# Strassen sums of a small weight written column block by column block, and a new order of work in the last block of queries

## The chip, the cores and the metric

The kernel runs on one core of a Trainium2 chip. The metric is the device time of one execution in microseconds (us); lower is better. All arithmetic is float32.

## The reference, cut to what matters

The layer is a gated cross-attention followed by an RMS norm. `x` is 8 x 1024 x 1024, the context 8 x 64 x 512, `W_mem` 1024 x 512, `W_gate` 1024 x 2048.

```python
memory_proj = einsum('bme,de->bmd', memory, W_mem)
scores = einsum('bnd,bmd->bnm', hidden_states, memory_proj) / sqrt(D)
attn = softmax(scores)
memory_context = einsum('bnm,bmd->bnd', attn, memory_proj)
gate = sigmoid(einsum('bnf,df->bnd', concat([hidden_states, memory_context]), W_gate) + b_gate)
fused = hidden_states + gate * memory_context
return fused * rsqrt(mean(fused ** 2) + 1e-6) * norm_w
```

The two large products are `memory_proj` (the setup) and the half of the gate that multiplies `hidden_states` (the main loop). The other half of the gate is folded into the setup: `memory_proj` is multiplied by the second half of `W_gate` once.

## The kernel before, in words

**Setup (about the first 82 us).** `W_mem` arrives transposed in the tile `wm`, four row blocks of 128 (the contraction) by 1024 output features. The feature of chunk j, position m is column `8*m + j`, so that the columns of one chunk lie 8 elements (32 bytes) apart. `transpose_mem(g)` transposes the context on TensorE into `memT`, VectorE and ScalarE copying half of the results each (L199). The product is one level of Strassen in the Winograd form, seven products of `pm_product`, each of 8 matmuls (the trace has two records for each): `split` gives the four blocks w11, w12 (row blocks 0-1 and 2-3, chunks 0-3) and w21, w22 (chunks 4-7). VectorE forms the left sums `ps1` = w21+w22, `ps2` = ps1-w11, `ps3` = w11-w21, `ps4` = w12-ps2 with the helper `tt` (L95); in the trace ps1 to ps3 are `pm_s`, ps4 and the right sums `pt1`, `pt2` are `pm_it`, and the results of the products (`pm`) are added into `mpT` and `pm_t`. The products run in the order 1 (w11), 2 (w12), 5 (ps1), 6 (ps2), 7 (ps3), 3 (ps4), 4 (w22). The weights of a matmul are

```python
mm(o, l[:, k, :, j], r[:, k, :], j % 2 == 0 and k == 0, k == 1)
```

with `l` laid out as `[P, 2, P, KH]` (k, m, j): for a sum the 128 columns of a weight load lie 4 elements (16 bytes) apart, for a block read straight from `wm` 8 elements (32 bytes). Then follow seven `mg_product`s (`pg` in the trace) of `memory_proj` with the second half of `W_gate`. Meanwhile SyncE's queue stores `mpT` (`mpd`), loads the first block of `x` (`load_xq`, tile `xq`, which takes over the memory of `wm`), and VectorE transposes it into the tiles `a` (L333).

**Main loop (16 blocks of 512 rows, "quads" q).** Each quad is seven outer Strassen products in `ORDER` 1, 6, 7, 5, 4, 2, 3, each of seven inner products in "slots" named A, B, C, D, A again, E, F (tiles kA to kF). A quad has 49 slots. `at(slot, fn)` hangs a piece of other work on a slot: it is emitted just before that slot's matmuls. So the order of instructions on each engine is fixed by hand, and each engine works through its own list in that order. Within an outer product ScalarE copies kA to `u` (L783) and VectorE adds kB, kC, kD to it (`u<-u,kB` and so on); the second A product writes kA again and so waits for that copy. The last four outer products (5, 4, 2, 3) also form the attention context `pc` (rows d = odd and c = even tiles of 128 rows) and finish the gate: `sigmoid` on ScalarE, then `gated` on VectorE (multiply by `pc`).

**The last quad** finishes differently. `last_gated` multiplies by `pc`, adds `x` (tile `xl`), and has ScalarE square and sum half a row block (`junk`, L701); `last_root` adds the two half sums on VectorE and takes the root on ScalarE (`halves`, L707); `last_norm` takes the reciprocal, scales (L717) and stores. `sqrt_table()` loads the root's function table ahead of its last use.

**In the first quad** VectorE also forms the sums of the weight blocks of outer products 2 and 3 (`inner_sum`, `it<-w`, four 128x512 operations for each), at slots 3 to 6 and 10 to 13. The softmax of the quad's scores lies at slots 10 (`softmax_a`) and 13 (`softmax_b`), and TensorE transposes its result (`pa`, L427) at slot 18.

Of the kernel before, what the change touches and what calls it, by code (L numbers as in the profile page):

```python
# [8 lines left out]
F32 = mybir.dt.float32  # L9
AF = mybir.ActivationFunctionType  # L10
ALU = mybir.AluOpType
# [4 lines left out]
P = 128  # L16
# [4 lines left out]
def tile_gated_cross_attention_rmsnorm(  # L21
# [42 lines left out]
    nc = tc.nc  # L64
    B, N, D = x.shape
# [5 lines left out]
    KD = D // P  # L71
    KE = E // P
    H = 512
    C = 256
# [4 lines left out]
    const = ctx.enter_context(tc.tile_pool(name="const", bufs=1))  # L79
# [4 lines left out]
    small = ctx.enter_context(tc.tile_pool(name="small", bufs=1))  # L84
# [4 lines left out]
    pin = tc.keep_in_program_order  # L89

    def mm(o, lhsT, rhs, start, stop):
        pin(nc.tensor.matmul(o, lhsT, rhs, start=start, stop=stop, skip_group_check=True))  # L92

    def tt(eng, o, a, b, op):
        pin(eng.tensor_tensor(o, a, b, op))  # L95

    def load(o, i):
        pin(nc.sync.dma_start(o, i))

    def t4k(pool, shape, tag, name):  # L100
        return pool.tile(shape, F32, tag=tag, name=name)
# [33 lines left out]
    for k in range(KD):  # L135
        t = t4k(*((gpool, [P, D], "gate") if k < 7 else (apool, [P, D], "s4")), f"w2_{k}")
# [42 lines left out]
    eps_sb = const.tile([P, 1], F32, name="eps_sb")  # L179
# [7 lines left out]
    def transpose_mem(g):  # L187

        cols = slice(g * (BM // 2), (g + 1) * (BM // 2))
        for k in range(KE):  # L190
            for r in range(2):
                n = 2 * g + r
                pin(
                    nc.tensor.transpose(
                        pt[k][:, n * P : (n + 1) * P], memq[g][:, r, k * P : (k + 1) * P], ident
                    )
                )
            o = memT[k // 2][:, k % 2, cols]
            pin((nc.scalar.copy if k % 2 else nc.vector.tensor_copy)(o, pt[k][:, cols]))  # L199
# [1 line left out]
    pt = [bank(4, [P, BM], "pt0")]  # L201
    pt += [ps_ctx.tile([P, BM], F32, tag="ctx", name=f"pt{k}") for k in (1, 2)]
    pt += [ps.tile([P, BM], F32, tag="sc", name="pt3")]
    transpose_mem(0)


    def outer_sum(o, a, b, k=slice(0, 4)):
# [13 lines left out]
    KH = KD // 2  # L221
# [6 lines left out]
    def setup_bank(name):  # L228
        nonlocal setup_next
        tag = setup_banks[setup_next % 8]  # L230
        setup_next += 1
        return (ps_ctx if tag == "ctx" else ps).tile([P, H], F32, tag=tag, name=name)

    def split(t, r):

        return t.rearrange("p k (m j) -> p k m j", j=KD)[:, :, :, KH * r : KH * (r + 1)]

    def pm_left(pool, tag, name):
        return t4k(pool, [P, 2, P, KH], tag, name)

    def pm_product(n, l, r, k_first=False):

        pgs = [setup_bank(f"pm{n}_{i}") for i in range(2)]
        order = [(j, k) for j in range(KH) for k in range(2)]
        if k_first:
            order.sort(key=lambda jk: jk[1])
        for j, k in order:
            o = pgs[j // 2][:, (j % 2) * HM : (j % 2 + 1) * HM]
            mm(o, l[:, k, :, j], r[:, k, :], j % 2 == 0 and k == 0, k == 1)
        return pgs  # L250

    def pm_sum(o, a, pgs):
        for i in range(2):
            js = slice(2 * i, 2 * i + 2)
            pg = pgs[i].rearrange("p (j n) -> p j n", n=HM)
            tt(nc.vector, o[:, js], a[:, js], pg, ALU.add)

    w11, w12 = (split(wm[:, 2 * k : 2 * k + 2, :], 0) for k in range(2))
    w21, w22 = (split(wm[:, 2 * k : 2 * k + 2, :], 1) for k in range(2))
    e11, e12 = (memT[0][:, :, c * HM : (c + 1) * HM] for c in range(2))  # L260
    e21, e22 = (memT[1][:, :, c * HM : (c + 1) * HM] for c in range(2))
    pu = const.tile([P, KH, H], F32, tag="t5", name="pm_t5")[:, :, :HM]
    ps4 = const.tile([P, 3, 2, C], F32, tag="it5", name="pm_it5")[:, :2]
    ps4 = ps4.rearrange("p a k c -> p (a k c)").rearrange("p (k m j) -> p k m j", k=2, j=KH)
    ps1 = pm_left(apool, "s1", "pm_s1")
    ps2 = pm_left(apool, "s2", "pm_s2")
    ps3 = pm_left(small, "mg", "pm_s3")
    in_it7 = const.tile([P, 3, 2, C], F32, tag="it7", name="pm_it7")
    pt1, pt2 = in_it7[:, 0], in_it7[:, 1]

    p1 = pm_product(1, w11, e11, True)
    tt(nc.vector, ps1, w21, w22, ALU.add)
    transpose_mem(1)
    for i in range(2):
        pin(
            nc.scalar.copy(
                pu[:, 2 * i : 2 * i + 2], p1[i].rearrange("p (j n) -> p j n", n=HM)
            )
        )
    pgs = pm_product(2, w12, e21)  # L280
    tt(nc.vector, pt1, e12, e11, ALU.subtract)
    tt(nc.vector, ps2, ps1, w11, ALU.subtract)
# [30 lines left out]

    pgs = pm_product(3, ps4, e22)
    pm_sum(m21, m21, pgs)
    p4 = pm_product(4, w22, e21)


    A, S, L2, O = {}, {}, {}, {}
# [1 line left out]
    def where(q, t=0):  # L321
        return q // QPB, (q % QPB) * QT + t * P
# [254 lines left out]
    def at(slot, fn, *args):  # L577
        due.setdefault(slot, []).append(lambda: fn(*args))

    def mid(key, fn, *args):  # L580
        beside.setdefault(key, []).append(lambda: fn(*args))
# [40 lines left out]
    for o in (2, 3):  # L622
        w1_place(o)
    for i, (o, n) in enumerate((o, n) for o in (2, 3) for n in range(4)):
        at((3, 4, 5, 6, 10, 11, 12, 13)[i], inner_sum, nc.vector, o, n)
    slot = 0

    def step():
# [4 lines left out]
    def gated(q, t, h, pc):  # L633
        g = O[q, t][:, h * H : (h + 1) * H]
        tt(nc.vector, g, g, pc, ALU.mult)

    def sigmoid(q, t, h):
        g = O[q, t][:, h * H : (h + 1) * H]
        pin(nc.scalar.activation(g, g, AF.Sigmoid))  # L639
# [42 lines left out]
    xl, halves = {}, {}  # L682
# [8 lines left out]
    def last_gated(t, h, pc):  # L691
        q = NQ - 1
        gated(q, t, h, pc)
        cols = slice(h * H, (h + 1) * H)
        g = O[q, t][:, cols]
        tt(nc.vector, g, g, xl[t][:, cols], ALU.add)
        if t not in halves:
            halves[t] = t4k(small, [P, 3], f"halves{t}", f"halves{t}")
        junk = t4k(small, [P, H], "junk", f"junk_{t}_{h}")
        pin(  # L700
            nc.scalar.activation(junk, g, AF.Square, accum_out=halves[t][:, h : h + 1])  # L701
        )

    def last_root(t):
        ss = halves[t]
        tt(nc.vector, ss[:, 2:3], ss[:, 0:1], ss[:, 1:2], ALU.add)
        pin(nc.scalar.activation(ss[:, 2:3], ss[:, 2:3], AF.Sqrt, bias=eps_sb, scale=1.0 / D))  # L707

    def last_norm(t, h):
        b, n0 = where(NQ - 1, t)  # L710
        rstd = halves[t][:, 2:3]
        if h == 0:
            pin(nc.vector.reciprocal(rstd, rstd))
        cols = slice(h * H, (h + 1) * H)
        g = O[NQ - 1, t][:, cols]
        pin(
            nc.vector.scalar_tensor_tensor(g, g, rstd, nw_sb[:, cols], ALU.mult, ALU.mult)  # L717
        )
        load(out[b, n0 : n0 + P, cols], g)

    def sqrt_table():

        t = t4k(small, [P, 1], "warm", "warm")
        pin(nc.scalar.activation(t, eps_sb, AF.Sqrt))

    def outer_product(q, o, ext):
# [54 lines left out]
        p1, u2, u3, u4 = (ut[:, i, :] for i in range(4))  # L781
# [12 lines left out]
        pcs = []  # L794
        if ext:
            row, h, g = ext
# [28 lines left out]
        if ext:  # L825
            sigmoid(q, 2 * row + 1, h)
            last = q + 1 == NQ
            if last:
                at(slot + 1, last_gated, 2 * row + 1, h, pcs[1])
            else:  # L830
                at(slot + 1, gated, q, 2 * row + 1, h, pcs[1])
        product("F", 1, s4, R22, not ext)
        fin(1, "F", u4)
        if ext:
            sigmoid(q, 2 * row, h)
            if last:
                at(slot + 2, last_gated, 2 * row, h, pcs[0])
            else:
                at(slot + 2, gated, q, 2 * row, h, pcs[0])
        if o in (4, 3) and q + 1 == NQ:  # L840
            c, d = 2 * ext[0], 2 * ext[0] + 1
            if o == 3:
                sqrt_table()
            first = (4, 5) if o == 4 else (3, 3)
            at(slot + first[0], last_root, d)
            at(slot + first[1], last_root, c)
            for i, t in enumerate((d, c)):
                for h_ in range(2):
                    at(slot + first[1] + 1 + 2 * i + h_, last_norm, t, h_)
        elif o in (4, 3):  # L850

            row = ext[0]
            c, d = 2 * row, 2 * row + 1
            for t in (d, c):
                at(slot + 5, residual, q, t)
            if row == 0:
                when = (17, 18, 23, 29, None, None)
            else:
                when = (17, 18, 23, 25, 26, 28)
            at(slot + when[0], square, q, c)  # L860
            at(slot + when[1], square, q, d)
            for w_, (t, h_) in zip(when[2:], ((c, 0), (c, 1), (d, 0), (d, 1))):
                if w_ is None:
                    mid((q + 1, 4), norm, q, t, h_)
                else:
                    at(slot + w_, norm, q, t, h_)
# [7 lines left out]
    while due:  # L874
        slot = min(due)
# [27 lines left out]
```

## Time and profile before

| | |
|---|---|
| median of 3 runs | 979.76 us (979.5 to 979.79) |
| the profiled execution's own time | 979.91 us |
| its span in the profile | 978.1 us |
| granted TensorE clock, mean | 0.997 |
| busy share: TensorE matmul, weight load, VectorE, ScalarE, GpSimd | 99%, 79%, 85%, 33%, 77% |
| setup, to the first kA | 82.7 us |
| a quad of the main loop (weight loads of psT, 88.9 to 918.2 us, over 15 quads) | 55.3 us |

The profile shows one execution. Its span runs from the first to the last recorded instruction; 1.8 us of the execution's own time lie around it. Rows of a timeline give start, duration, engine, line, operation, output<-inputs, shape and count, with the idle time before and what ended it in brackets. PE is TensorE's matmuls, PEld its weight loads, DVE VectorE, ACT ScalarE, POOL GpSimd, SP the queue of SyncE.

### The profile page before, as it was taken

To read this page: it belongs to the slowest core of one execution; us is meant where nothing else is said; L and a number is where in the kernel's file an instruction comes from. 1 tells how busy PE (TensorE), PEld (TensorE's weight loads), DVE (VectorE), ACT (ScalarE), POOL (GpSimd) and SP (SyncE) were. 2 spreads that over 40 slices of the span, in tenths; PEclk is the share of its full clock that TensorE was granted. 3 is DMA by queue.
4 is the path that set the end of the run, shared out by engine and by line. 5 is a ranking of instruction groups with operands and counts; after the bars stand their busy time and mean duration, and the time that the engine had idled before them with its cause. 6 is when DMAs were issued, how large, how long until landed. Compare 5 with 4: busy or idle time off the path is not lost.

```text
span 978.1 us, 14392 instructions
## 1 busy us (share of the span) xinstructions
PE 964.3 (99%) x4986; PEld 776.3 (79%) x4986; DVE 827.0 (85%) x1487; ACT 323.0 (33%) x596; POOL 754.6 (77%) x895
## 2 busy tenths in 40 slices
PE   9999999999999999999999999999999999999995
PEld 8646888888888888888888888888888888888873
DVE  5988788979797988979797988979797988979787
ACT  1000234151423334151423334151423334151434
POOL 4986878878787878878787878878787878878772
PEclk9999999999999999999999999999999999999998
DMA  9856173482818373482819373482818373482612
GB/s 371 267 147 157 27 130 98 114 177 72 176 65 174 117 130 98 112 179 73 176 65 175 113 131 99 112 180 71 177 66 172 116 133 98 111 181 68 169 65 86
DMA packets 71255, 128.32 MB, mean 131 GB/s; under 512 B 12432, under 2 KB 49296, under 8 KB 70928
## 3 DMA queue, kind: packets, MB, share of 16 engines
q1 hardware_dynamic: 61760, 93.34, 35.1%
q0 software_dynamic: 9280, 33.56, 18.6%
q8 instruction: 39, 0.64, 0.3%
q10 hardware_dynamic: 144, 0.52, 0.2%
q14 instruction: 32, 0.26, 0.1%
HBM read 87.56 MB, written 39.85 MB: 130 GB/s over the span
## 4 chain that ended last, share of the span: by engine, by line
PE 95%; DVE 3%; DMA 1%; issue 0%; ACT 0%; POOL 0%; DVEq 0%; ACTq 0%
PE kA L92 19%; PE pc L92 12%; PE kE L92 11%; PE kF L92 10%; PE kD L92 10%; PE kC L92 10%; PE kB L92 10%; PE psT L92 6%; PE pg L92 5%; PE pm L92 3%; DVE gate L95 1%; DMA memq<-in_mem 1%; DVE gate L717 0%; PE pa L427 0%; PE sc L401 0%
## 5 line engine op out<-in xcount | busy, mean ns | idle before, releaser
L95 POOL TENSOR_TENSOR gate<-gate,u 128x256 f32<-128x256 f32 x336 | 270.3, 834 | 116.0 <-DVE u L95 110.4
L639 ACT ACTIVATE gate<-gate 128x512 f32<-128x512 f32 x128 | 79.0, 629 | 400.7 <-DVE gate L95 400.6
L95 POOL TENSOR_TENSOR l<-a 128x256 f32<-128x256 f32 x128 | 128.6, 1004 | 56.3 <-DVE a L95 55.5
L333 DVE STREAM_TRANSPOSE a<-xq 128x512 f32<-128x512 f32 x128 | 138.0, 1100 | 3.2 <-DMA mgd<-mpq 3.2
L92 PE MATMUL pc<-mg,attnT 64*128 64x256 f32 x512 | 127.4, 389 | 0.0
L668 DVE SCALAR_TENSOR_TENSOR gate<-gate,ss,nw_sb 128x512 f32<-128x512 f32 x120 | 126.2, 1061 | 1.1
L92 PE MATMUL kD<-it,l 128*128 128x256 f32 x448 | 115.0, 379 | 0.0
L92 PE MATMUL kB<-it,l 128*128 128x256 f32 x448 | 115.0, 379 | 0.0
L92 PEld LDWEIGHTS pc<-mg,attnT 64*128 64x128 f32 x512 | 90.6, 186 | 29.7 <-issue 21.2
L92 PE MATMUL kA<-w,a 128*128 128x256 f32 x384 | 98.7, 379 | 0.4 <-ACT u L783 0.4
L92 PEld LDWEIGHTS kD<-it,l 128*128 128x128 f32 x448 | 85.1, 190 | 11.6
L92 PEld LDWEIGHTS kB<-it,l 128*128 128x128 f32 x448 | 85.1, 190 | 11.6
L95 DVE TENSOR_TENSOR gate<-gate,pc 128x512 f32<-128x512 f32 x128 | 87.2, 681 | 5.8 <-ACT gate L639 5.8
L95 POOL TENSOR_TENSOR l<-s 128x256 f32<-128x256 f32 x96 | 75.6, 787 | 10.1 <-PE kF L92 10.0
L92 PEld LDWEIGHTS kA<-w,a 128*128 128x128 f32 x384 | 71.6, 190 | 10.2 <-ACT u L783 0.8
L783 ACT COPY u<-kA 128x256 f32<-128x256 f32 x112 | 40.5, 362 | 102.4 <-PE kA L92 100.4
L95 DVE TENSOR_TENSOR u<-u,kB 128x256 f32<-128x256 f32 x112 | 45.6, 407 | 28.2 <-PE kB L92 24.7
L92 PE MATMUL kE<-it,a 128*128 128x256 f32 x256 | 69.0, 392 | 0.0
L92 PE MATMUL kA<-t,s 128*128 128x256 f32 x256 | 67.4, 386 | 0.0
L92 PE MATMUL kF<-w,l 128*128 128x256 f32 x256 | 65.7, 379 | 0.0
L92 PE MATMUL kC<-w,l 128*128 128x256 f32 x256 | 65.7, 379 | 0.0
L653 ACT ACTIVATE junk<-gate 128x1024 f32<-128x1024 f32 x60 | 63.5, 1059 | 1.4 <-DMA gate<-in_x 0.5
(138 smaller groups left out, 2034.2 us busy)
## 6 DMA issues: line engine op xcount, KB each, us to landing
xq<-in_x SPq DMA_DIRECT2D x64, 512.0 KB, 9.7
gate<-in_x POOLq DMA_DIRECT2D x60, 512.0 KB, 8.2
out<-gate SPq DMA_DIRECT2D x60, 512.0 KB, 2.6
w<-in_w_gate_t SPq DMA_DIRECT2D x8, 512.0 KB, 11.0
w<-in_w_gate_t SPq DMA_DIRECT2D x2, 2048.0 KB, 17.0
mg<-mgd SPq DMA_DIRECT2D x16, 256.0 KB, 3.8
mpd<-mpT SPq DMA_DIRECT2D x4, 512.0 KB, 6.5
mgd<-mpq SPq DMA_DIRECT2D x16, 128.0 KB, 4.4
```

Source lines behind the costliest of these rows:

```text
L92: pin(nc.tensor.matmul(o, lhsT, rhs, start=start, stop=stop, skip_group_check=True))
L95: pin(eng.tensor_tensor(o, a, b, op))
L333: nc.vector.transpose(A[key][:, :, r * P : (r + 1) * P], chunks(xq[q][:, 4 * t : 4 * t + 4, :], KD)[:, half * KH : (half + 1) * KH],)
L639: pin(nc.scalar.activation(g, g, AF.Sigmoid))
L653: nc.scalar.activation(junk, O[q, t], AF.Square, accum_out=ss[:, t % 2 : t % 2 + 1])
L668: nc.vector.scalar_tensor_tensor(g[:, cols], g[:, cols], rstd[:, t % 2 : t % 2 + 1], nw_sb[:, cols], ALU.mult, ALU.mult,)
L783: pin(nc.scalar.copy(p1, kb["A"]))
```

## The change

Three things are changed.

1. **Layout of W_mem's blocks.** `split` returns the blocks as (k, j, m), and the tiles of the sums are laid out so. VectorE now reads the blocks of `wm` with a step of 32 bytes and writes the sums so that the 128 columns of one chunk are adjacent. ScalarE copies two blocks into the same layout: the first row block of w11 (`pw11`, a 128x512 copy ahead of `transpose_mem(0)`), and w22 (`pw22`, two such copies behind the copies of product 1). Product 1's second row block and product 2 still read `wm`.
2. **First quad.** The four weight sums of outer product 3 move from slots 10-13 to slots 22-25.
3. **Last quad.** `last_gated` is hung one slot later. The square of the first half of a row is followed on ScalarE by an Identity with scale 1/D and bias eps into the third column of `halves`; `last_root` is then a single root on ScalarE, with that column as its bias, and its VectorE addition is gone. Roots and norms of both row pairs get other slots.

```diff
     def split(t, r):
-        return t.rearrange("p k (m j) -> p k m j", j=KD)[:, :, :, KH * r : KH * (r + 1)]
+        return t.rearrange("p k (m j) -> p k j m", j=KD)[:, :, KH * r : KH * (r + 1), :]
     def pm_left(pool, tag, name):
-        return t4k(pool, [P, 2, P, KH], tag, name)
+        return t4k(pool, [P, 2, KH, P], tag, name)
...
-            mm(o, l[:, k, :, j], r[:, k, :], j % 2 == 0 and k == 0, k == 1)
+            mm(o, l[k][:, j, :], r[:, k, :], j % 2 == 0 and k == 0, k == 1)
...
-    transpose_mem(0)
...
-    p1 = pm_product(1, w11, e11, True)
+    in_it1 = const.tile([P, 3, 2, C], F32, tag="it1", name="pm_it1")
...
+    pin(nc.scalar.copy(pw11, w11[:, 0]))
+    transpose_mem(0)
+    p1 = pm_product(1, (pw11, w11[:, 1]), e11, True)
...
+    for k in range(2):
+        pin(nc.scalar.copy(pw22[:, k], w22[:, k]))
     pgs = pm_product(2, w12, e21)
...
-    p4 = pm_product(4, w22, e21)
+    p4 = pm_product(4, pw22, e21)
...
-        at((3, 4, 5, 6, 10, 11, 12, 13)[i], inner_sum, nc.vector, o, n)
+        at((3, 4, 5, 6, 22, 23, 24, 25)[i], inner_sum, nc.vector, o, n)
...
     def last_gated(t, h, pc):
...
+        pin(nc.scalar.activation(junk, g, AF.Square, accum_out=ss[:, h : h + 1]))
+        if h == first:
+            pin(nc.scalar.activation(ss[:, 2:3], ss[:, h : h + 1],
+                                     AF.Identity, bias=eps_sb, scale=1.0 / D))
     def last_root(t):
-        tt(nc.vector, ss[:, 2:3], ss[:, 0:1], ss[:, 1:2], ALU.add)
-        pin(nc.scalar.activation(ss[:, 2:3], ss[:, 2:3], AF.Sqrt, bias=eps_sb, scale=1.0 / D))
+        pin(nc.scalar.activation(ss[:, 2:3], ss[:, h : h + 1],
+                                 AF.Sqrt, bias=ss[:, 2:3], scale=1.0 / D))
...
-                at(slot + 1, last_gated, 2 * row + 1, h, pcs[1])
+                at(slot + 2, last_gated, 2 * row + 1, h, pcs[1])
...
-                at(slot + 2, last_gated, 2 * row, h, pcs[0])
+                at(slot + 3, last_gated, 2 * row, h, pcs[0])
...
-            first = (4, 5) if o == 4 else (3, 3)
-            at(slot + first[0], last_root, d)
-            at(slot + first[1], last_root, c)
-            for i, t in enumerate((d, c)):
-                for h_ in range(2):
-                    at(slot + first[1] + 1 + 2 * i + h_, last_norm, t, h_)
+            when = (4, 5, 7, 9, 11, 12) if o == 4 else (2, 4, 5, 6, 7, 8)
+            at(slot + when[0], last_root, d)
+            at(slot + when[1], last_root, c)
+            for w_, (t, h_) in zip(when[2:], ((d, 0), (d, 1), (c, 0), (c, 1))):
+                at(slot + w_, last_norm, t, h_)
```

More of the change, by code (lines that the diff above doesn't have):

```diff
@@ L234, in split @@
     def split(t, r):
-        return t.rearrange("p k (m j) -> p k m j", j=KD)[:, :, :, KH * r : KH * (r + 1)]
+        return t.rearrange("p k (m j) -> p k j m", j=KD)[:, :, KH * r : KH * (r + 1), :]
     def pm_left(pool, tag, name):
-        return t4k(pool, [P, 2, P, KH], tag, name)
+        return t4k(pool, [P, 2, KH, P], tag, name)
     def pm_product(n, l, r, k_first=False):
         pgs = [setup_bank(f"pm{n}_{i}") for i in range(2)]
+        if not isinstance(l, tuple):
+            l = l[:, 0], l[:, 1]
         order = [(j, k) for j in range(KH) for k in range(2)]
@@ L263, in tile_gated_cross_attention_rmsnorm @@
     ps4 = const.tile([P, 3, 2, C], F32, tag="it5", name="pm_it5")[:, :2]
-    ps4 = ps4.rearrange("p a k c -> p (a k c)").rearrange("p (k m j) -> p k m j", k=2, j=KH)
+    ps4 = ps4.rearrange("p a k c -> p (a k c)").rearrange("p (k j m) -> p k j m", k=2, j=KH)
     ps1 = pm_left(apool, "s1", "pm_s1")
@@ L269, in tile_gated_cross_attention_rmsnorm @@
     pt1, pt2 = in_it7[:, 0], in_it7[:, 1]
-    p1 = pm_product(1, w11, e11, True)
+    in_it1 = const.tile([P, 3, 2, C], F32, tag="it1", name="pm_it1")
+    pw22 = in_it1[:, :2].rearrange("p a k c -> p (a k c)").rearrange(
+        "p (k j m) -> p k j m", k=2, j=KH
+    )
+    pw11 = in_it1[:, 2].rearrange("p k c -> p (k c)").rearrange("p (j m) -> p j m", j=KH)
+    pin(nc.scalar.copy(pw11, w11[:, 0]))
+    transpose_mem(0)
+    p1 = pm_product(1, (pw11, w11[:, 1]), e11, True)
     tt(nc.vector, ps1, w21, w22, ALU.add)
@@ L697, in last_gated, with last_root @@
         if t not in halves:
-            halves[t] = t4k(small, [P, 3], f"halves{t}", f"halves{t}")
+            halves[t] = t4k(small, [P, 3], f"halves{t}", f"halves{t}"), h
+        ss, first = halves[t]
         junk = t4k(small, [P, H], "junk", f"junk_{t}_{h}")
-        pin(
-            nc.scalar.activation(junk, g, AF.Square, accum_out=halves[t][:, h : h + 1])
-        )
-    def last_root(t):
-        ss = halves[t]
-        tt(nc.vector, ss[:, 2:3], ss[:, 0:1], ss[:, 1:2], ALU.add)
-        pin(nc.scalar.activation(ss[:, 2:3], ss[:, 2:3], AF.Sqrt, bias=eps_sb, scale=1.0 / D))
+        pin(nc.scalar.activation(junk, g, AF.Square, accum_out=ss[:, h : h + 1]))
+        if h == first:
+            pin(
+                nc.scalar.activation(
+                    ss[:, 2:3], ss[:, h : h + 1], AF.Identity, bias=eps_sb, scale=1.0 / D
+                )
+            )
+    def last_root(t):
+        ss, first = halves[t]
+        h = 1 - first
+        pin(
+            nc.scalar.activation(
+                ss[:, 2:3], ss[:, h : h + 1], AF.Sqrt, bias=ss[:, 2:3], scale=1.0 / D
+            )
+        )
     def last_norm(t, h):
         b, n0 = where(NQ - 1, t)
-        rstd = halves[t][:, 2:3]
+        rstd = halves[t][0][:, 2:3]
         if h == 0:
```

## The prediction

> **What bounds the kernel now.** I read first the page's chain, then TensorE's weight loads through the setup, then VectorE beside them, and last the two ends.
>
> ```profile
> PE 95%; DVE 3%; DMA 1%; issue 0%; ACT 0%; POOL 0%; DVEq 0%; ACTq 0%
> ```
>
> TensorE is 95% of the chain. Time is gained only where TensorE runs slower than its pace, where it waits, or after its last matmul at about 967.5 us. The weight loads in order of time show the first:
>
> ```profile
> 11.80 3.91 PEld L92 LDWEIGHTS pm<-memT,wm 128*128 128x128 f32 x16
> 15.62 7.57 PEld L92 LDWEIGHTS pm<-pm_it,pm_s 128*128 128x128 f32 x32
> 23.09 3.85 PEld L92 LDWEIGHTS pm<-memT,pm_s 128*128 128x128 f32 x16
> 26.85 3.83 PEld L92 LDWEIGHTS pm<-memT,pm_it 128*128 128x128 f32 x16
> 30.59 3.93 PEld L92 LDWEIGHTS pm<-memT,wm 128*128 128x128 f32 x16
> 34.42 0.42 PEld L92 LDWEIGHTS pg<-w,mpT 128*128 128x128 f32 x2
> ...
> 84.23 0.84 PEld L92 LDWEIGHTS kC<-w,l 128*128 128x128 f32 x4
> 85.09 0.84 PEld L92 LDWEIGHTS kD<-it,l 128*128 128x128 f32 x4
> ```
>
> No idle time stands between these rows, so the distance of starts is the pace. Products 5, 6, 7, 3 take 30.59 - 15.62 = 14.97 us for 64 records, 0.234 each; product 4 takes 3.83 for 16, 0.239. The kC row, of the same shape, takes 0.86 for 4, 0.2155. The step between weight columns is the difference I see. VectorE in the setup:
>
> ```profile
> 11.29 1.22 DVE L95 TENSOR_TENSOR pm_s<-wm 128x1024 f32<-128x1024 f32 x1 [3.88 <-DMA wm<-in_w_mem_t]
> ...
> 21.66 0.69 DVE L95 TENSOR_TENSOR pm_t<-pm_t,pm 128x512 f32<-128x512 f32 x1 [0.34 <-PE pm L92]
> 23.52 0.69 DVE L95 TENSOR_TENSOR pm_t<-pm_t,pm 128x512 f32<-128x512 f32 x1 [1.18 <-PE pm L92]
> ...
> 27.28 0.69 DVE L95 TENSOR_TENSOR mpT<-mpT,pm 128x512 f32<-128x512 f32 x1 [1.19 <-PE pm L92]
> ...
> 54.09 4.10 DVE L333 STREAM_TRANSPOSE a<-xq 128x512 f32<-128x512 f32 x4 [3.25 <-DMA mgd<-mpq]
> ...
> 82.92 0.69 DVE L95 TENSOR_TENSOR mg_c<-mg_c,pg 128x512 f32<-128x512 f32 x1 [0.64 <-PE pg L92]
> ```
>
> VectorE waits for TensorE 0.34 + 1.18 + 1.19 us before 28 us; then it is full but for the wait at 54.09 (for `xq`, whose load SP issues at 39.30 behind the store of the last `mpT`) and 0.64 at 82.92. It is the second-tightest engine. At the end, ScalarE and TensorE:
>
> ```profile
> 960.78 0.63 ACT L701 ACTIVATE junk<-gate 128x512 f32<-128x512 f32 x1 [1.42 <-DVE halves L713]
> 961.32 0.19 ACT L701 ACTIVATION_READ_ACCUMULATOR junk<-gate 128x1 f32 x1
> 961.41 0.35 ACT L783 COPY u<-kA 128x256 f32<-128x256 f32 x1
> ...
> 961.82 1.13 PE L92 MATMUL kA<-w,s 128*128 128x256 f32 x4 [1.08 <-ACT u L783]
> ```
>
> The copy of kA stands behind a square that waits for VectorE, and the second A product waits for the copy.
>
> [...] No run here shows a TENSOR_TENSOR with a 32-byte step. [...]
>
> **Setup, TensorE.** Adjacent columns for 88 of the 112 records: products 5, 6, 7, 3: 14.97 - 64 x 0.2155 = 1.18; product 4: 3.83 - 3.45 = 0.38; the first half of product 1: 8 x (0.236 - 0.2155) = 0.16. The other half and product 2 keep their pace. Together -1.7 us.
>
> **Setup, VectorE.** The sums ps1 to ps4 now read with a 32-byte step. The nearest row is L333: its STREAM_TRANSPOSE reads at that step, 1.10 us for 512 columns, 2.0 ns each. I take 2.1 us a sum against 1.22, +0.9[...]. [...] At +0.9, ps1 ends 0.9 later and pt1 at about 14.7, ahead of product 5 (15.5); pt2 at 18.3 ahead of product 6 (18.9); ps3 at 21.8 ahead of 7 (22.4); ps4 at 24.2, 2.9 late, ahead of 3 (25.8). From there VectorE need not wait any more: the 2.7 us of waits shown above take the delay, and the last `mpT` is done at 38.8, as before. So the `xq` load, and the whole of VectorE to 82.3, stand where they did. TensorE now wants the bank of kC at 82.8; `mg_c` releases it at 82.3. The cover is 0.5 us. GpSimd's work behind pt1 slips 1.8 us and has 3.0 us idle at 70 us. Beyond 4 x 0.9 + 0.5 = 4.1 us added to VectorE, the gain is lost one for one. I book 0.2 against it: **-1.5 us**, ends -1.7 and 0[...].
>
> **Setup, ScalarE.** `pw11` waits for the first piece of `wm`, landed 4.5 us after its issue at 0.74, so 5.24; behind it wait both memT copies, which began at 6.76. A 128x512 copy takes 0.60 at L276; doubled for the step, 1.2, it ends at 6.4. Cost 0; at 2 us it would cost 0.5. `pw22` runs from 13.5 in a stretch where ScalarE is idle for 24.9 us, and is needed at 29: 0. GpSimd's first write of the reused tile `it1` (38.7) waits for product 4, done by 33: 0. SP's `xq` load now waits for the copies too: 0.
>
> **First quad.** `pa` comes 1.17 us after kD's start at 101.42; in the second quad 0.87. Four sums of 0.68 to 1.23 delayed the softmax: -0.3. At slots 22-25 they push 3.3 us into VectorE, which waits there 0.65 + 0.37 + 0.44; the transposes and kD's additions then end near 114.2, and the next kB needs that bank at 114.5. The sums' own readers come at slot 42. Cover 0.3, little: **-0.2 us**, ends -0.35 and +0.6.
>
> **Last quad.** The copy now precedes the square. Second A products against kD's start + 0.86: 943.35 - 943.01, 952.22 - 951.69, 961.82 - 960.57: 0.34 + 0.53 + 1.25 = 2.1. In product 3, kD's context matmul waited for `u<-u,kD` until 964.92, due at 964.28: 0.6 more. Late next is VectorE: queued behind the moved `gated` and norms are `u<-u,kC`, `u<-u,kD` and the kE, kF additions. Stepping its new list with the old durations, the wait of 1.11 us at 952.20 fills, `u<-u,kD` of product 3 ends at 962.1 for a need at 962.2, and c's multiplication frees its context bank at 961.15 for a need at 961.75. I book half of the 0.6: **-2.4 us**, ends -2.8 and -1.0. The four norms of the first row pair take their four stores on SP with them; each lands in 2.0 us, long before the end. POOL's list is unchanged.
>
> **Tail.** Before, square d ends at 970.86, square c at 971.62, the two additions and roots follow, and the first reciprocal stands at 971.83. Now d's root (0.3, L707) follows its square, and the reciprocal at about 971.2; four norms of 0.7 run on. Two Identities of 0.3 lie in idle ScalarE time. **-0.5 us**, ends -0.7 and 0.
>
> Sum: -1.5 - 0.2 - 2.4 - 0.5 = -4.6. The profiled execution took 979.91 (span 978.1 and 1.8 around it), 0.15 above the median; from the median, **975.2 us**.
>
> **Rivals.** (1) VectorE becomes the setup's bound[...]; 976.7. For it: VectorE is full from 28 us on; against it: the L333 row. (2) The last quad trades waits: VectorE, full there, holds kD or a context bank, only 1.0 of 2.4 is gained; 976.6, with (1) 978.1. (3) The weight step does not set the pace: the 0.234 stays, -3.1 remains, 976.7. Against it: all else is alike. (4) Slower: the stepped read is far dearer than any row. Past 4.1 us every us is TensorE's; the others' gains are used up when the four add 4.1 + 4.8 = 8.9, that is 3.4 us a sum, and at 4.0 us a sum it is 982.
>
> **Chances.** Likeliest 0.55 (974.0 to 976.3); (1) 0.17, (2) 0.13, (3) 0.05, together and with small losses still mostly below 977.8; (4) 0.04; the rest a mix. A measurement here tells 0.2%, 2 us: faster 0.87, same 0.09, slower 0.04. Range 973.6 to 977.8, from all the best ends (-6) to (1) and part of (2).
>
> **What would show it.** pm's weight loads at 0.2155 but for 24 records; `pm_s<-wm` near 2.1 us; the wait at 54.09 still there; first kA near 81; `pa` 0.87 behind kD; no second A waiting for ScalarE; last norm's end some 3 us nearer to the first kA than before. Wrong: a TensorE wait for VectorE before 83 us or in the last 40.

## The result, and the profile after

The changed kernel takes 974.35 us in the median (974.07 to 974.66, 6 runs) against 979.68 for the kernel before, timed beside it: 5.3 us less, a ratio of 0.9946 (95% interval 0.9933 to 0.9958). The forecast was 975.2, range 973.6 to 977.8. The profiled execution took 974.45 us, span 972.7.

Read at the same places of both traces, the difference builds up like this (psT is the product for a quad's scores; it comes once in every quad, at the same place):

| place in the trace | before, us | after, us | difference so far | of this stage |
|---|---|---|---|---|
| first kA (end of the setup) | 82.72 | 80.91 | -1.81 | -1.81 |
| psT of the second quad (end of the first) | 144.24 | 142.24 | -2.00 | -0.2 |
| start of the last kF (15 more quads) | 966.51 | 961.66 | -4.85 | -2.85 |
| end of the last norm | 974.96 | 969.50 | -5.46 | -0.6 |
| span | 978.1 | 972.7 | -5.4 | 0 |

The first weight load of product 1 starts at 7.02 us in the one and 7.03 in the other. In all traces it lies between 6.64 and 7.29, with the old layout and with the new; from it to the first kA the two other traces with the old setup take 75.69 us, like before (75.70), and the traces with the changed setup 73.86 to 73.95 (after: 73.88). So the -1.81 does not hang on this one pair.

The table of the kernel before gives 55.3 us for a quad. That figure counts up to the last weight load of the last psT; from first load to first load a quad takes 55.1 us on average, in before as in after.

First the chain of the page of after, which was 95% TensorE and 3% VectorE:

```profile
PE 99%; DVE 0%; ACT 0%; DVEq 0%; issue 0%
```

The stretches of VectorE that stood in the chain, in the first and in the last quad, are gone. TensorE's weight loads in the setup, in order of time:

```profile
15.34 6.90 PEld L92 LDWEIGHTS pm<-pm_it,pm_s 128*128 128x128 f32 x32
22.27 3.43 PEld L92 LDWEIGHTS pm<-memT,pm_s 128*128 128x128 f32 x16
25.72 6.88 PEld L92 LDWEIGHTS pm<-memT,pm_it 128*128 128x128 f32 x32
32.63 0.41 PEld L92 LDWEIGHTS pg<-w,mpT 128*128 128x128 f32 x2
```

From 15.34 to 32.63 are 17.29 us for 80 records, 0.216 each: the same five products took 18.80 in before. Another 0.28 comes from product 1. VectorE's dearer sums did not reach TensorE:

```profile
11.02 2.04 DVE L95 TENSOR_TENSOR pm_s<-wm 128x1024 f32<-128x1024 f32 x1 [3.51 <-DMA wm<-in_w_mem_t]
...
19.89 2.01 DVE L95 TENSOR_TENSOR pm_it<-wm,pm_s 128x1024 f32<-128x1024 f32 x1
53.30 4.11 DVE L344 STREAM_TRANSPOSE a<-xq 128x512 f32<-128x512 f32 x4 [3.14 <-DMA mgd<-mpq]
81.11 0.69 DVE L95 TENSOR_TENSOR mg_c<-mg_c,pg 128x512 f32<-128x512 f32 x1 [0.86 <-PE pg L92]
```

A sum with the 32-byte step takes 2.04 us, the wait for `xq` is still there, and at 81.11 VectorE waits for TensorE, not the other way round. In the last quad and the tail:

```profile
955.90 0.35 ACT L803 COPY u<-kA 128x256 f32<-128x256 f32 x1
957.04 0.63 ACT L712 ACTIVATE junk<-gate 128x512 f32<-128x512 f32 x1 [0.79 <-DVE gate L95]
```

```profile
957.58 1.03 PE L92 MATMUL kA<-w,s 128*128 128x256 f32 x4
```

```profile
966.37 0.16 DVE L733 RECIPROCAL halves<-halves 128x1 f32<-128x1 f32 x1 [0.41 <-ACT halves L724]
...
968.09 1.41 DVE L737 SCALAR_TENSOR_TENSOR gate<-gate,halves,nw_sb 128x512 f32<-128x512 f32 x2
```

The copy of kA now comes ahead of the square that waits, and the second A product has no bracket: it does not wait.

### The profile page after: what moved, and what is told of

It is laid out like the page before. It is cut to its first block, busy times and chain, and to the rows that moved or that the text cites. A ratio compares the mean times of both kernels' runs of the same rounds, so it can differ in the third digit from the quotient of the medians.

```text
span 972.7 us, 14393 instructions
## 1 busy us (share of the span) xinstructions
PE 961.5 (99%) x4986; PEld 772.9 (79%) x4986; DVE 825.1 (85%) x1483; ACT 327.0 (34%) x603; POOL 763.4 (78%) x895
## 4 chain that ended last, share of the span: by engine, by line
PE 99%; DVE 0%; ACT 0%; DVEq 0%; issue 0%
PE kA L92 20%; PE pc L92 12%; PE kE L92 11%; PE kD L92 10%; PE kF L92 10%; PE kC L92 10%; PE kB L92 10%; PE psT L92 6%; PE pg L92 5%; PE pm L92 3%; PE pz L92 0%; PE sc L412 0%; PE pa L438 0%; PE pt L194 0%; DVE gate L737 0%; ACT L744 0%
## 5 line engine op out<-in xcount | busy, mean ns | idle before, releaser
L95 POOL TENSOR_TENSOR l<-a 128x256 f32<-128x256 f32 x128 | 132.1, 1032 | 55.6 <-DVE a L95 55.6
L92 PEld LDWEIGHTS kD<-it,l 128*128 128x128 f32 x448 | 85.1, 190 | 11.6
## 6 DMA issues: line engine op xcount, KB each, us to landing
w<-in_w_gate_t SPq DMA_DIRECT2D x8, 512.0 KB, 10.9
```

## The experiments

My theory was that the three parts of the change act apart, each at its own place. The first three runs take one part each; they showed that this is not so, and most of the later runs look for the reason.

### One part at a time

**The layout alone.** The kernel after with slots and last quad of before:

```diff
-        at((3, 4, 5, 6, 22, 23, 24, 25)[i], inner_sum, nc.vector, o, n)
+        at((3, 4, 5, 6, 10, 11, 12, 13)[i], inner_sum, nc.vector, o, n)
...  (last_gated, last_root, last_norm and their slots as before the change)
```

> The kernel before with the layout and the two ScalarE copies alone; first and last quad as before. If the parts add up as the traces read, the first kA starts 1.8 us earlier (80.9 us) and nothing else moves: 977.9 us. If the setup's gain is given back later, because VectorE with its dearer sums holds the first quad, kA is early but the psT of the second quad is not (144.2 us): 979.5 us or more.

Measured: median 981.74, ratio 1.0013 (1.0006 to 1.0019). The executions fall into three groups: 978.0 to 978.2 (3 of 20), 980.4 to 980.5 (5), 981.7 to 982.2 (12). Neither expectation had groups. Only the shortest shows what the setup brings; the first profile was of such a run (977.97).

**The last quad alone.** The kernel before with the change's hunks for the last quad:

```diff
-                at(slot + 1, last_gated, 2 * row + 1, h, pcs[1])
+                at(slot + 2, last_gated, 2 * row + 1, h, pcs[1])
-                at(slot + 2, last_gated, 2 * row, h, pcs[0])
+                at(slot + 3, last_gated, 2 * row, h, pcs[0])
...  (last_gated, last_root, last_norm and their slots as in the change)
```

> The kernel before with the last quad's order and roots alone. If the parts add up: the last kF starts 2.85 us earlier (963.7 us) and the end 3.4 us earlier: 976.3 us. If the last quad gains only because everything ahead of it came earlier, below 1 us: 979 us.

Measured: 976.46 (976.03 to 976.74), ratio 0.9968 (0.9956 to 0.998), as expected. TensorE no longer waits for ScalarE; from the second psT to the last kF it gains 2.9 us.

**The first quad alone.** The kernel before with the four sums at the later slots:

```diff
-        at((3, 4, 5, 6, 10, 11, 12, 13)[i], inner_sum, nc.vector, o, n)
+        at((3, 4, 5, 6, 22, 23, 24, 25)[i], inner_sum, nc.vector, o, n)
```

> The kernel before with the four weight sums moved to slots 22 to 25 alone. If they held the softmax: pa 0.87 us behind kD and the psT of the second quad 0.2 to 0.35 us earlier, 979.4 us. If the move only trades that wait for one of kB on VectorE in the fifth product: no change, 979.7 us.

Measured: 979.44, ratio 0.9998 (0.999 to 1.0006), not to be told from before. The first quad goes from 55.39 to 55.15 us from psT to psT, the 0.2 that the prediction had.

So the parts alone are worth most often +2.1, -3.2 and -0.2, and together they are worth -5.3.

### What the layout alone runs into

The same kernel again, for a profile of a longer execution:

> The kernel with the layout alone, once more, for a profile of one of its longer executions: its times lay at 978.0, 980.5 and 981.8 to 982.2 us, and the profile shown was of the shortest. If the longer ones lose their time in the first quad, where VectorE now comes later to the softmax, the psT of the second quad is 2.5 to 4 us later than 142.3 us and the rest is alike. If it is lost all over the loop (GpSimd and VectorE holding each other), the quads are 0.2 us longer each.

Measured: 982.08 (980.41 to 982.59), ratio 1.002 (1.0013 to 1.0027). The profiled run took 980.53: its first quad took 57.49 us (before: 55.39), the thirteen behind it 55.05 each and the next 55.28, as in before (55.31). A third profile caught a run of the longest group:

> The layout alone once more, for a profile of another of its times: 977.97 was profiled with VectorE's second input sum at 0.85 us, 980.53 with 3.68 us for it. If GpSimd's hold makes all its times, an execution near 982 has this sum, or it and the next (the sum into w), held for over 4 us in all, and the first quad 58.5 to 59.5 us from psT to psT. If the longest times come from elsewhere, the first quad is at most 57.5 us and the loss stands in a later quad.

Measured: 981.71, first quad 59.18 us, as expected. The sum itself took hardly longer than in the run of 980.53, though (3.83 against 3.68); a second loss comes with it. VectorE and GpSimd in this run:

```profile
95.68 3.83 DVE L95 TENSOR_TENSOR it<-w,it 128x512 f32<-128x512 f32 x1
99.43 0.41 DVE L95 TENSOR_TENSOR gate<-gate,kA 128x256 f32<-128x256 f32 x1
99.76 0.41 DVE L95 TENSOR_TENSOR gate<-gate,kD 128x256 f32<-128x256 f32 x1
```

```profile
94.56 2.37 POOL L95 TENSOR_TENSOR gate<-gate,u 128x256 f32<-128x256 f32 x3
96.62 0.98 POOL L95 TENSOR_TENSOR l<-a 128x256 f32<-128x256 f32 x1
97.30 0.97 POOL L95 TENSOR_TENSOR l<-a,l 128x256 f32<-128x256 f32 x1
97.98 0.96 POOL L95 TENSOR_TENSOR l<-s 128x256 f32<-128x256 f32 x1
99.02 1.06 POOL L95 TENSOR_TENSOR l<-l,s 128x256 f32<-128x256 f32 x1
```

The second weight sum, 0.68 us elsewhere, takes 3.83: it is held up while GpSimd works without a gap. It ends at 99.51, about one normal length behind the first gap in GpSimd's row of work (97.98 + 0.96 = 98.94, next start 99.02). Behind it in VectorE's list stand `gate<-gate,kA` and `gate<-gate,kD`. The second of them frees the bank of the next kB: it ends at 100.17, and kB starts at 100.22. TensorE, matmuls:

```profile
96.87 1.03 PE L92 MATMUL kA<-w,a 128*128 128x256 f32 x4
100.22 2.08 PE L92 MATMUL kB<-it,l 128*128 128x256 f32 x4 [2.32 <-DVE gate L95]
```

Four matmuls of kB take 2.08 us behind the wait, twice the usual 1.03. The table by stretches gives the reason in the column PEclk, the third from the end:

```profile
98.00:99.00 1.00, 0.00 (x0) 0.00 (x0) 1.00 (x1) 0.36 (x1) 0.94 (x2) 1.00 1.29 225
...
100.00:101.00 1.00, 0.78 (x2) 0.69 (x3) 1.00 (x3) 0.00 (x0) 0.09 (x1) 0.50 0.04 8
102.00:103.00 1.00, 1.00 (x4) 0.73 (x3) 0.93 (x5) 0.00 (x0) 0.00 (x0) 0.50 0.00 0
104.00:105.00 1.00, 1.00 (x7) 0.85 (x7) 0.56 (x2) 0.12 (x1) 0.71 (x2) 1.00 0.00 0
```

The granted clock falls to 0.50 at 99.97, 2.08 us after the end of the last matmul (97.89), and is back at 1.00 at 103.38, 3.41 us later. In the run of 980.53 the same sum took 3.68 us and TensorE waited 2.18, but the clock stayed at 1.00. In the run of 977.97 the sum got in between two of GpSimd's:

```profile
95.73 0.85 DVE L95 TENSOR_TENSOR it<-w,it 128x512 f32<-128x512 f32 x1
```

This accounts for all three groups: not held, held (+2.3), held with the clock lowered (+1.5 more). The mean granted clock of every execution of this kernel bears it out: 0.997 in all eleven at 980.4 to 980.7, and 0.994 or 0.995 in all 25 from 981.7 on.

In the run of 981.71 both operands of the held sum lie in SBUF. It waited through several of GpSimd's operations up to GpSimd's first pause, of 0.08 us at 98.94. The two sums behind it, which read PSUM, were not stretched: `gate<-gate,kA` and `gate<-gate,kD` took 0.41 each beside GpSimd's sum at 99.02.

What separates the cases is small. Where the sum slipped in, it started 1.39 us behind the start of GpSimd's `gate` sums (before: 1.40); in the two runs where it was held, 1.27 and 1.12. Four traces show that the cases go with these tenths, not that they decide. Why the new layout shifts the two engines by them was not settled.

**The layout with the sums moved, old last quad.** If that is the cause, moving the four sums away must cure it:

```diff
-        at((3, 4, 5, 6, 10, 11, 12, 13)[i], inner_sum, nc.vector, o, n)
+        at((3, 4, 5, 6, 22, 23, 24, 25)[i], inner_sum, nc.vector, o, n)
```

> The kernel after with the last quad of before: the new layout of W_mem's sums and the four input sums of the first quad at slots 22 to 25, nothing else. It asks why the layout alone, with those sums at slots 10 to 13, came out at 978.0 to 982.2 us. My theory: at the old slots one of those sums, VectorE reading two operands from SBUF, falls among GpSimd's sums and is held by them (3.68 us for 0.68 in the profile at 980.5), and the sum that gives TensorE its bank back stands behind it. With the four sums away the loss is gone in every run: 974.35 + 3.2 for the last quad and tail (the last quad alone was worth 3.22) = 977.6, spread under 0.7, second psT in the profile near 142.2. Rival A, the parts add: 981.7 - 0.24 = 981.5. Rival B, the loss comes of the layout and the old last quad together (GpSimd's or SyncE's order late in the kernel): 980 or more, several groups of times, and the first quad not longer than 55.3 us in the profile.

Measured: 977.82, ratio 0.9982 (0.9975 to 0.9989); 19 of 21 executions lie between 977.5 and 978.2; the other two, at 979.0, have no profile. The groups at 980.4 and 982 are gone, and the profiled run's first quad takes 55.05 us. Beside the layout, the move is worth 3.9 to 4.3 us in the median and not 0.2. In after, too, an operation is held at this place, but one that has time:

```profile
97.42 1.73 DVE L95 TENSOR_TENSOR e<-e,den 128x256 f32<-128x256 f32 x1
```

The softmax's division, 0.42 us elsewhere, ends at 99.15, and `pa` needs it at 100.47.

### The setup: step and cover

**Sums in the old layout, copies kept.** The sums are laid out (k, m, j) as before, so the 64 weight loads of products 5, 6, 7 and 3 have the step of 16 bytes again; the ScalarE copies stay.

```diff
-        return t4k(pool, [P, 2, KH, P], tag, name)
+        return t4k(pool, [P, 2, P, KH], tag, name).rearrange("p k m j -> p k j m")
...
-    tt(nc.vector, ps1, w21, w22, ALU.add)
+    tt(nc.vector, mj(ps1), mj(w21), mj(w22), ALU.add)      # ps2 to ps4 likewise
...  (the tile of ps4 likewise)
```

> The changed kernel with the four sums in the old layout (16-byte step between weight columns) and the two copies kept. If the step sets TensorE's pace: 64 of the records at 0.234 again, 1.2 us later, 975.5 us, and the sums at 1.22 us again. If the setup's gain has another source (the transposes behind the copy, earlier landings): 974.4 us.

Measured: 975.48 (975.3 to 975.74), 1.13 more than after, as expected; from product 1's first weight load to the first kA it takes 75.01 us, also 1.13 more. The weight loads of products 5 to 7 are back at the old pace:

```profile
15.10 7.57 PEld L92 LDWEIGHTS pm<-pm_it,pm_s 128*128 128x128 f32 x32
22.57 3.85 PEld L92 LDWEIGHTS pm<-memT,pm_s 128*128 128x128 f32 x16
```

These sums cost VectorE 1.22 us again where nothing holds them, so VectorE is not what slows TensorE here. The step between weight columns sets TensorE's pace here, 0.234 us a load at 16 bytes against 0.216 for neighbours; rival 3 is out.

**Chunks in pairs.** The columns of two chunks stay beside each other, so VectorE reads two neighbours at a time, each sum in two operations (one for a row block), and the 128 columns of a weight load lie 8 bytes apart:

```diff
-            mm(o, l[k][:, j, :], r[:, k, :], j % 2 == 0 and k == 0, k == 1)
+            mm(o, l[k][:, j // 2, :, j % 2], r[:, k, :], j % 2 == 0 and k == 0, k == 1)
...  (`split`, the tiles of the sums and of the copies, and the four sums to match)
```

> The changed kernel with the sums laid out in pairs of chunks: weight columns 8 bytes apart[...]; VectorE reads runs of two elements, row block by row block. [...] TensorE's pace stays 0.2155, a sum takes two operations of 0.68 instead of one of 2.03, and the time is as after, 974.4 us. If any step costs: pace 0.234, 975.9 us.

Measured: 974.81 (974.53 to 975.35), ratio 0.995: 0.46 above after in the median, with ranges that overlap. TensorE's weight loads:

```profile
15.29 6.91 PEld L92 LDWEIGHTS pm<-pm_it,pm_s 128*128 128x128 f32 x32
22.22 3.43 PEld L92 LDWEIGHTS pm<-memT,pm_s 128*128 128x128 f32 x16
25.67 6.89 PEld L92 LDWEIGHTS pm<-memT,pm_it 128*128 128x128 f32 x32
32.58 0.41 PEld L92 LDWEIGHTS pg<-w,mpT 128*128 128x128 f32 x2
```

Products 5 to 4 take 17.29 us for 80 records, as in after: a step of 8 bytes cost TensorE nothing here. The first sum costs VectorE 1.29 us instead of 2.04; the other three, beside GpSimd's sums, take 2.37 to 3.42. Neither matters, since VectorE does not hold TensorE up.

**One sum four times.** The line of `ps4` stands four times.

```diff
     tt(nc.vector, ps4, w12, ps2, ALU.subtract)
+    tt(nc.vector, ps4, w12, ps2, ALU.subtract)             # three times
```

> The changed kernel with ps4 formed four times over: 6.1 us more on VectorE in the setup. If VectorE is the second-tightest engine there and the cover is what the trace after shows (waits of 0.18 and 0.97 us for TensorE, then 2.4 us between mg_c's end at 80.3 and the kC that needs its bank): 6.1 - 3.5 = 2.6 us later, 977.0 us. With the cover of the prediction (0.5 us and the waits): 978.8 us. If only the product that reads ps4 waits (2.2 us) and VectorE catches up: 976.5 us.

Measured: 982.65 (980.62 to 983.92), ratio 1.0027: 8.3 us more than after, beyond every expectation, for three operations of 2.03 us each. VectorE, and TensorE's loads:

```profile
21.23 11.59 DVE L95 TENSOR_TENSOR pm_it<-wm,pm_s 128x1024 f32<-128x1024 f32 x4
```

```profile
22.38 3.43 PEld L92 LDWEIGHTS pm<-memT,pm_s 128*128 128x128 f32 x16
32.94 8.96 PEld L92 LDWEIGHTS pm<-memT,pm_it 128*128 128x128 f32 x32 [7.13 <-issue]
```

The four take 2.9 us each, where `ps4` took 2.01 in after. GpSimd's four sums `t_w<-w` now run beside them and take 11.64 us, in after 4.96; the first starts 1.3 us later than in after. The last ends 10.9 us later (32.82 against 21.90). Product 3 began at 25.72 in after, so `ps4` had 3.8 us to spare, and TensorE waits for the other 7.1. Then the lowered clock comes again: 0.50 from 30.58 to 37.41, which is 6.83 us, and the 32 loads take 8.96 us instead of 6.88. 7.1 + 2.1 is most of the 9.5 us that psT is late in this run (983.71 us). The six executions spread over 3.3 us, and only this one has a profile. So the cover is real, and in this run the delay past it cost more than its length: 9.5 us for a wait of 7.1.

### The last quad

**The old slots of last_gated.** After, with the multiplications by `pc` one slot earlier again:

```diff
-                at(slot + 2, last_gated, 2 * row + 1, h, pcs[1])
+                at(slot + 1, last_gated, 2 * row + 1, h, pcs[1])
-                at(slot + 3, last_gated, 2 * row, h, pcs[0])
+                at(slot + 2, last_gated, 2 * row, h, pcs[0])
```

> The changed kernel with last_gated back on its old slots; new roots and norms kept. If the place of the square ahead of the copy of kA is the cause: second A products wait for ScalarE again, 2.1 to 2.8 us are lost, 976.5 to 977.2 us. If the leaner roots and the spread norms, which take four additions off VectorE, are the cause: at most 0.7 us are lost, 975.0 us.

Measured: 978.27, ratio 0.9986 (0.9979 to 0.9992): 3.9 of the 5.3 us are gone, more than expected. From the second psT to the last kF it loses 2.7, within the expectation; TensorE waits for ScalarE again at the second A of three products:

```profile
941.16 1.13 PE L92 MATMUL kA<-t,a 128*128 128x256 f32 x4 [0.47 <-ACT u L803]
949.99 1.13 PE L92 MATMUL kA<-w,a 128*128 128x256 f32 x4 [0.31 <-ACT u L803]
959.16 1.13 PE L92 MATMUL kA<-w,s 128*128 128x256 f32 x4 [0.66 <-ACT u L803]
```

Another 1.3 are lost in the tail, which I had left out: the last square comes later, and the last pair of norms begins 7.7 us behind the last kF's start instead of 6.4. So this one slot carries the whole gain of the last quad; without it the leaner roots and the spread norms gain nothing (978.27, against 977.82 with the whole of the old last quad).

**Two of the last four norms on ScalarE.** After, with GpSimd multiplying two early halves by the norm weights, and ScalarE scaling them at the end; the order of the four norms is changed to match:

```diff
+        if (t, h) in weighted:
+            pin(nc.scalar.activation(g, g, AF.Copy, scale=rstd))
...
+        tt(nc.gpsimd, g, g, nw_sb[:, cols], ALU.mult)      # tiles 1 and 0, left half
...
```

> The kernel after, with the last four norms shared: GpSimd multiplies the two halves that are early (tiles 1 and 0, left columns) by the norm weights while TensorE does its last products, and at the end ScalarE scales those two by the root's reciprocal while VectorE norms the other two. In after the chain at the end is ScalarE's second square 966.24, its root 966.98 to 967.28, VectorE's reciprocal 967.90 behind two norms, then two norms to 969.50. Theory: VectorE's norms end at 968.2 and ScalarE's second scale, 0.6 each from 967.3, at 968.5; the end comes 1.0 us earlier, 973.4. Rival A: GpSimd's two products of 1.27 us hold VectorE's norm at 961.45 or its residual at 963.95 and the tail gains nothing or loses up to 1 us, 974.4 to 975.4. Rival B: the scale on ScalarE takes 1.1 us a half and the end stands at about 969.5, 974.4.

Measured: 975.58 (974.85 to 975.6), 1.2 slower than after: rival A. VectorE and GpSimd in the last quad:

```profile
961.79 1.79 DVE L740 SCALAR_TENSOR_TENSOR gate<-gate,halves,nw_sb 128x512 f32<-128x512 f32 x1
```

```profile
961.76 2.94 POOL L95 TENSOR_TENSOR gate<-gate,nw_sb 128x512 f32<-128x512 f32 x2
```

GpSimd starts 0.03 us ahead of a norm that takes 0.75 elsewhere; beside GpSimd's two products, 2.94 together, the norm takes 1.79. The sum of kE behind it comes 1.0 us late against the last kF, and with it the first of the last four stores: its data move from 7.4 us behind the last kF's start on, 6.5 in after. The last norm does end 0.1 us sooner against the last kF than in after, but the four stores follow one another without a gap and end 0.7 us later. The other 0.3 us of this profile's longer span lie ahead of the last kF. As in the first quad, a VectorE operation on SBUF operands is stretched beside GpSimd's work, here by 1.04 us.

**One norm, timed past the collision.** GpSimd does one half only and first waits for that norm, by a product of one column:

```diff
+        tt(nc.gpsimd, mark, O[NQ - 1, 2][:, H : H + 1], nw_sb[:, 0:1], ALU.mult)
+        g = O[NQ - 1, t][:, 0:H]
+        tt(nc.gpsimd, g, g, nw_sb[:, 0:H], ALU.mult)
...  (the same scale on ScalarE; the other tile's reciprocal ahead of the second norm)
```

> The kernel after, with one of the last four norms on ScalarE: GpSimd multiplies tile 0's left half by the norm weights, and waits first for VectorE's last norm of tile 2 (a product of one column), so that its 1.27 us fall where VectorE reads only PSUM beside SBUF: 962.2 to 963.5 on after's scale. The reciprocal of tile 0 moves ahead of tile 1's second norm. If what cost the two-norm version was GpSimd's hold on that norm (1.79 us for 0.75), the sum of kE ends at 962.5 as in after, VectorE's three last norms end at 968.9, ScalarE's scale before that, and the end comes 0.6 us sooner: 973.75 (973.5 to 974.1). If VectorE is held all the same (the residual at 963.95, or sums that read PSUM too), or the scale is late, 974.3 to 975.6.

Measured: 974.38 (974.24 to 974.62), the same as after. The hold is gone (that norm 0.74), and the norms do end 0.7 us nearer to the last kF. But the stores do not. What all DMA engines move from 964 us on, in 40 slices of 0.35 us, in this kernel and then in after:

```profile
GB/s 0 0 0 0 0 0 0 0 0 0 0 369 357 82 386 375 404 375 386 263 0 0 0 0 0 0 0 0 23 0 0 0 0 0 0 0 0 0 0 0
```

```profile
GB/s 0 0 0 0 0 0 0 0 0 0 0 35 369 375 375 339 246 374 386 392 106 0 0 0 0 0 0 0 0 23 0 0 0 0 0 0 0 0 0 0
```

Four stores of 256 KB leave at about 380 GB/s, 0.7 us each, one behind the other. In after only a slight dip stands between them; with the norms sooner, the last three run without one. The data end 0.2 us sooner in a profile whose last kF is itself 0.3 sooner. The gain in the norms is given back to the row of stores. No kernel tried beats after beyond what can be measured.

## Why the prediction was right, point by point

**Setup, TensorE and VectorE: right.** Booked -1.5, measured -1.81. The loads run at 0.216 as worked out, a sum takes 2.04 (2.1 estimated), and TensorE waits for none; product 1 gave 0.28 where 0.16 was booked. The 0.2 held back for VectorE was not needed. The prediction set all four sums against 1.22 and so added 3.6 us; they added only 2.0, since the old `ps3` and `ps4` had already been stretched to 1.39 and 2.29. So `ps4` ended at 21.90 and not at 24.2. The cover at the end of the setup was mis-sized with it: `mg_c` was done at 80.26 for a kC that started at 82.64, 2.4 us where the prediction had 0.5. GpSimd's memT sums were stretched instead, from 2.11 and 1.28 to 3.53 and 5.03, without effect. The `pw11` copy took 1.12 us (1.2 estimated) and cost nothing: behind it ScalarE waited 0.80 for TensorE's transposes.

**First quad: right in sum, its mechanism mis-sized.** The quad gained 0.2, as booked (`pa` 0.86 behind kD), and kB's bank came when it was due, with no cover left (112.30, kB at 112.35). The 0.2 is one reading: the quad takes 55.37 to 55.39 us in the traces with the sums at slots 10 to 13 where the second of them slips in, and 55.05 to 55.32 in those with the sums moved. The step that failed is "Four sums of 0.68 to 1.23 delayed the softmax: -0.3". I took 1.23 and 0.85 as what these sums cost. They were a sum of 0.68 and a hold, and the hold had no fixed length here: with it the sum took 0.85, 3.68 and 3.83 at the same place. So a part that I priced at 0.2 keeps 3.9 to 4.3 us from being lost once the layout has shifted the engines. The prediction added up the parts; that the total came out right although this term was mis-sized is luck in so far as the prediction did not see that the setup's gain hangs on this part. The change makes all of them.

**Last quad: right, the size a little off.** Booked -2.4, measured -2.85. The term is the 0.6 of kD's context matmul, of which I booked half: its wait is down to 0.13 us (a wait of 0.14 stands now at the same place of product 4). All three waits of the second A are gone, 2.1, and with them the slower first matmuls behind each (1.13 us for the four of kA, now 1.03).

**Tail: right.** -0.6 for -0.5; the reciprocal and norms follow the squares as described.

**Rivals.** (1) did not come: a sum took 2.04 us, and TensorE waited for none; that it could be much dearer was a guess, which the trace of before did not show. (2), traded waits, did not come: waits of 0.13 and 0.14 us at kD's context matmuls are all that is left. (3) fell with the sums in the old layout. (4), the slower side, has its mechanism: in the run with `ps4` four times, the last of them 10.9 us late, VectorE passes its cover and the kernel is slower than before. In that run the loss is not one for one, as I had it, but higher, because the clock is lowered during the wait.

## What to carry to other kernels

A row that is longer than its like can be a hold and not a cost (here 0.85, 3.68 and 3.83 us for a sum of 0.68): look at what GpSimd does in the same microseconds before pricing it, and keep VectorE's operations on two SBUF inputs away from unbroken rows of GpSimd's work when TensorE waits for what is queued behind them (2.18 and 2.32 us here). Parts of a change that shift two engines against each other need not add; time them in pairs too. Where the stores follow one another without a gap, faster arithmetic ahead of them can be given back (here the norms ended 0.7 us nearer to the last kF, and the data of the stores did not).

## What the runs showed of the hardware

- A VectorE sum of two SBUF operands, 0.68 us elsewhere, took 3.68 and 3.83 in two runs of the layout alone: it was held for 3.0 to 3.2 us over several GpSimd operations, until GpSimd's first gap of 0.08 us. In two traces where it took 0.85 (before, and the shortest run of the layout alone) it had started 0.1 to 0.3 us later against GpSimd's row. In the run with `ps4` four times four sums of each engine ran beside one another in 11.6 us: 2.9 us each, against 2.01 for VectorE's and 1.24 for GpSimd's in after.
- A standstill of TensorE of 2.3 us went with a granted clock of 0.50 for 3.41 us in one run (it fell 2.08 us after the last matmul); one of 2.2 us in another run did not. With a standstill of 6.8 us, in the run with `ps4` four times, the clock was at 0.50 for 6.83 us, twice as long. What decides whether a wait is charged so was not shown.
- VectorE read 1024 columns at a step of 32 bytes in 2.01 to 2.05 us in after, whether one or both sources had the step, against 1.22 for neighbours four at a time (before) and 1.29 in pairs (two operations, the run with chunks in pairs). ScalarE copied 512 columns at that step in 1.12 us (after).
- Weight columns 8 bytes apart loaded like neighbours, at 0.216 us a load (the run with chunks in pairs, and after); 16 bytes apart took 0.234 and 32 bytes 0.239 (before).
